# Reordering the first and the last token blocks of a fused attention and feed-forward layer on one core

## The chip, the cores and the metric

The kernel runs on one core of a Trainium2 chip. The metric is the device time of one execution in microseconds. The kernel before takes 528.72 us as the median of 3 runs (527.85 to 529.94). A profile of one further execution is the source of every duration used below.

## The reference

The input is x, 4 x 2048 tokens of 256 features in float32, treated here as 8192 tokens. One layer is computed:

```python
Q, K, V = x @ W_q.T, x @ W_k.T, x @ W_v.T
# chunks of 32 tokens, mask[i, j] = decay ** (i - j) for i >= j, else 0
S = einsum('bncd,bnkd->bnck', Qc, Kc) * mask
O = einsum('bnck,bnkd->bncd', S, Vc)
out = (sigmoid(x @ W_g.T) * O) @ W_o.T + x
h = layernorm(x + out)
gate, up = h @ wg.T, h @ wu.T            # int weights times 1/127, hidden size 768
y = (silu(gate) * up) @ wd.T
result = layernorm(h + y)
```

`decay` is the sigmoid of one scalar that arrives by DMA.

## The kernel before, in words

The 8192 tokens are cut into 16 blocks of 512 (`TB`), numbered 0 to 15. All blocks run through the same stages, written out by Python without a hardware loop. `in_turn` and `in_steady_turn` pin an instruction's place in the program order of its engine; unpinned ones are placed by a scheduler when the program is built, so every engine's stream is fixed before the kernel runs.

**Products in three passes.** Most matrix products split both operands into `hi`, `lo` and `gap` parts (`weight_parts`, `weight_up`, `weight_gap`, `token_parts`, L436 to L490). `three` (L526) first issues the hi and lo products of both of its PSUM banks, scales each bank by `WHOLE` on ScalarE (L536), and later, when the caller calls the function it returned, issues the gap products (the third pass) and the finishing copy. In what follows "the first passes" are the hi and lo products and "the gap pass" is the third. The tiles are `p_g` (the gate product), `p_v` (V), `p_y` (x times W_q.T W_k, used for the scores) and `p_o` (the output projection). GpSimd makes the lo parts (L452, L476), VectorE the gaps of tokens (L482).

**Per block.** `attn_scores` (tile `ps`, L647) multiplies yT with xT on TensorE and the mask on VectorE into `sT`; `attn_values` (tile `po`, L669) multiplies with V, and VectorE applies the gate into `goT`. `split_out` adds the residual, and `moments` (L341, L342) takes mean and variance. The norm is applied on ScalarE by `normalize` (L429), from a scale and a shift that either come from a Sqrt on ScalarE (`root`, L350) and a reciprocal on VectorE, or, in `iterated_scale_and_shift` (L404 to L418), from a power and one Newton step on GpSimd alone. A Sqrt on ScalarE costs two table loads, one before it and one in `back_to_silu` (L940). The normed block is transposed: by TensorE in `transpose_h` (tile `pt`) for blocks 0 and 15, otherwise by `move_h` (L781, L788), which transposes 32 x 32 squares on VectorE and then issues 16 DMAs on SP's queue, tile `hT`, and `split_h` (L805, L806).

**Feed-forward.** `ffn_up` (L823 to L846) runs 6 chunks of 128 hidden features per block: 8 matmuls into `fg` and `fu`, a Silu on ScalarE (`s`), a product on VectorE (`u`), a rounded copy on ScalarE (`u_hi`, L845) and its remainder on GpSimd (`u_lo`, L846). `ffn_down` (tile `fdn`) multiplies u with the third weight; with `chunkwise` it takes the first four chunks of both banks first ("early") and the last two after that ("late").

**Head.** Before the data arrive, matmuls of zeros warm TensorE up (tile `pi`, L190, widths in `WARM`). Block 0's gate, V and y products are plain float32 (`pg`, `pv`, `py`). `make_mask` (L255 to L270) raises the decay to 0..31 by repeated squaring, 18 small VectorE operations behind the 15 that prepare the bits, into `chunk_mask` and `mask`. Block 0's norm uses `root` and then four VectorE operations on h (L922). The integer weights are cast by `cast_fg`, `cast_fu`, `cast_fd` on ScalarE, three operations of about 0.55 us to a call.

**Loop.** For b = 0 to 13, block b's feed-forward chunks are interleaved with block b+2's attention and block b+3's first products.

**Tail.** Iteration b = 13 has no block b+3. After it, blocks 14 and 15 run their feed-forward parts, the last four groups of tokens are normed one after another, and the stores end the kernel.

Of the kernel before, what the change touches and what calls it, by code (L numbers as in the profile page):

```python
# [54 lines left out]
P = 128  # L55
# [14 lines left out]
SHIFT = 2.0**12  # L70
TOP = 1.0 - 0.5 / SHIFT
WHOLE = 1.0 + 1.0 / SHIFT
WARM = 512, 512, 128


@with_exitstack
def kernel(
# [32 lines left out]
    sums = ctx.enter_context(tc.tile_pool(name="sums", bufs=1))  # L110
    small = ctx.enter_context(tc.tile_pool(name="small", bufs=8))
    psum = ctx.enter_context(tc.tile_pool(name="psum", bufs=8, space=bass.MemoryType.PSUM))

    def bank(name):
        return psum.tile([P, TB], F32, tag="ps", name=name)
# [116 lines left out]
        )  # L232
    chunk_mask = const.tile([P, CHUNK], F32, tag="chunk_mask", name="chunk_mask")
    nc.vector.tensor_scalar(chunk_mask, diff, 0.0, None, ALU.is_ge)
    bits = []
    for i in range(CHUNK.bit_length() - 1):
        bit_int = setup.tile([P, CHUNK], I32, tag="bit_int", name=f"bit_int_{i}")
        nc.vector.tensor_scalar(
            bit_int, diff, i, 1, ALU.logical_shift_right, ALU.bitwise_and
        )  # L240
        bit, factor = (
            setup.tile([P, CHUNK], F32, tag=f"{tag}_{i}", bufs=1, name=f"{tag}_{i}")
            for tag in ("bit", "factor")
        )
        nc.vector.tensor_copy(bit, bit_int)
        nc.vector.tensor_scalar(factor, bit, -1.0, 1.0, ALU.mult, ALU.add)
        bits.append((bit, factor))
    mask = const.tile([P, NG, PAIR], F32, tag="mask", name="mask")
    nc.vector.memset(mask, 0.0)

    def in_turn(ins):
        tc.keep_in_program_order(ins)

    def make_mask():
        in_turn(nc.scalar.activation(decay, decay, AF.Sigmoid))  # L255
# [73 lines left out]
    def in_steady_turn(ins):  # L329
        if steady:  # L330
            tc.keep_in_program_order(ins)
# [4 lines left out]
    def moments(r, name, groups=range(NG), order=free, mv=None):  # L336

        mv = no_moments(name) if mv is None else mv
        for g in groups:
            st = small.tile([P, 6], F32, tag="st", name=f"st_{name}_{g}")  # L340
            order(nc.vector.bn_stats(st, r[:, g, :]))  # L341
            order(nc.vector.bn_aggr(mv[:, g, :], st))  # L342
        return mv
# [9 lines left out]
        )  # L353
        return std

    def layer_norm(r, name, on_r=1.0, on_dst=1.0):


        mv = moments(r, name)
        rstd = root(mv, name, on_r)  # L360
        nc.vector.reciprocal(rstd, rstd)
        if on_dst != on_r:
            nc.vector.tensor_scalar(rstd, rstd, on_dst / on_r, None, ALU.mult)
        for g in range(NG):
            nc.vector.tensor_scalar(
                r[:, g, :],
                r[:, g, :],
                mv[:, g, 0:1],
                rstd[:, g : g + 1],
                ALU.subtract,  # L370
                ALU.mult,
            )
# [343 lines left out]
    def attn_residual(b, goT):  # L716

        xn = xns.pop(b)
        r = norm.tile([P, NG, D], F32, tag="h", name=f"h_{b}")

        def residual(gs, pb):
            in_steady_turn(nc.vector.tensor_tensor(flat(r, gs), pb, flat(xn, gs), ALU.add))

        project_back(b, (chunked(goT),), (chunked(given["wo"]),), residual, "pa")
        return r

    def attn_out(b, goT):
        r = attn_residual(b, goT)
        layer_norm(r, f"a{b}", on_r=HALF, on_dst=H_UP)
        return r  # L730

    def split_out(b, go_parts):

# [75 lines left out]
        return hi, lo  # L809


    def ffn_up(b, hT, uT, chunks, cols=slice(0, TB), held=False):

        n = cols.stop - cols.start
        for hc in chunks:
# [14 lines left out]
                        in_turn(product)  # L830
            s = work.tile([P, n], F32, tag="s", name=f"s_{b}_{hc}")
            in_turn(nc.scalar.activation(s, pg, AF.Silu, scale=SCALE / H_UP))  # L832
            if len(uT[0]) == hc:
                for kind, dtype, tiles in zip(("hi", "lo"), (F32R, F16), uT):
                    tiles.append(
                        acts.tile([P, TB], dtype, tag=f"u_{kind}", name=f"u_{kind}_{b}_{hc}")
                    )

            def multiply(hc=hc, pu=pu, s=s):
                u = work.tile([P, n], F32, tag="u", name=f"u_{b}_{hc}")  # L840
                in_steady_turn(
                    nc.vector.scalar_tensor_tensor(u, pu, U_UP / H_UP, s, ALU.mult, ALU.mult)  # L842
                )
                hi, lo = uT[0][hc][:, cols], uT[1][hc][:, cols]
                in_steady_turn(nc.scalar.copy(hi, u))  # L845
                nc.gpsimd.tensor_tensor(lo, u, hi.bitcast(F32), ALU.subtract)  # L846

            if held:
                return multiply
# [81 lines left out]

    table = const.tile([P, 1], F32, tag="table", name="table")
    given = {"wg": wg, "wv": wv, "wo": wo}
    hs, hTs = {}, {}

# [3 lines left out]

    weight_parts(wg, "wg", ("wg_hi", "wg_lo"))
    make_mask()
    weight_parts(wv, "wv", ("wv_hi", "wv_lo"))
    back_to_silu()
    sg, gate = attn_gate(0)
    x_parts, x_gaps = token_parts(xTs[1], "x_1")

    def with_m():
        make_m()  # L950
        given["m"] = m_sb
        weight_parts(m_sb, "m", ("wq", "wk"))

    v, copies = attn_v(0, with_m)
    weight_up("wg")
    gate()
    copies()
    yT = attn_y(0)
    weight_gap("wg")
    weight_up("wv")  # L960
    weight_gap("wv")
    in_turn(nc.scalar.mul(wo, wo, HALF**2))
    weight_parts(wo, "wo", ("wo_hi", "wo_lo"))
# [4 lines left out]
    fg, cast_fg = integers(ffn_gT, ffn_int[0], "fg")  # L968
    fu, cast_fu = integers(ffn_uT, ffn_int[1], "fu")
    fd, cast_fd = integers(ffn_dT, ffn_int[2], "fd")  # L970
    cast_fg(0)
    v_1, rest = split_v(1, x_parts)
    look_up([0])
    cast_fg(1)
    sT = attn_scores(0, yT)
    xTs[2] = load_xT(2)
    g_rest()
# [1 line left out]
    look_up([1, 2])  # L979
    yT, rest = split_y(1, x_parts)  # L980
    goT = attn_values(0, sT, v, sg)
    rest()
    cast_fu(0)
    x_parts, x_gaps = token_parts(xTs[2], "x_2")
    hs[0] = attn_residual(0, goT)
    sT_1 = attn_scores(1, yT)
    xTs[3] = load_xT(3)
    mv = moments(hs[0], "a0", order=in_turn)
    weight_up("wo")
    weight_gap("wo")  # L990
    std = root(mv, "a0", HALF, order=in_turn)
    back_to_silu()
    v, rest = split_v(2, x_parts)
    x_gaps()
    goT = attn_values(1, sT_1, v_1, sg_1)
    in_turn(nc.vector.reciprocal(std, std))
    in_turn(nc.vector.tensor_scalar(std, std, H_UP / HALF, None, ALU.mult))
    for g in range(NG):
        scaled(hs[0], g, mv, std)
    go_parts, go_gaps = token_parts(goT, "go_1")  # L1000
    cast_fu(1)
    rest()
    yT, rest = split_y(2, x_parts)
    hTs[0] = transpose_h(0, hs[0])
    go_gaps()
    rest()
    look_up([3])
    hs[1], out_rest = split_out(1, go_parts)
    sg, g_rest = split_gate(2, x_parts)
    cast_fd(0)  # L1010
    scales_h = iterated_scale_and_shift(out_rest(), of_h, "h_1")
    ahead = yT, v, sg


# [7 lines left out]
    for b in range(NB - 2):  # L1022
# [7 lines left out]
        if b:  # L1030
            normalize(hs[b + 1], *scales_h)
        up_now(b, hT, uT, 0)
        if b == 0:
            g_rest()
            cast_fd(1)
            x_parts, x_gaps = token_parts(xTs[m], f"x_{m}")
        up_now(b, hT, uT, 1)
        if b:
            moving = move_h(b + 1, hs[b + 1])
        sT = attn_scores(n, yT)  # L1040
        if m + 1 < NB:
            xTs[m + 1] = load_xT(m + 1)
        up_now(b, hT, uT, 2)
        if b == 0:
            x_gaps()
            normalize(hs[b + 1], *scales_h)
            moving = move_h(b + 1, hs[b + 1])
        if more:
            v_next, v_rest = split_v(m, x_parts)
            up_now(b, hT, uT, 3)  # L1050
            v_rest()
            if scales_out is not None:
                normalize(r_before, *scales_out)
                store(b - 2, r_before)
        goT = attn_values(n, sT, v, sg)
        if b == 0:
            look_up(range(4, n_pieces))
        if b == 1:
            count = count_wide()
            n_wide_early = const.tile([1, 1], I32, tag="n_wide_early", name="n_wide_early")  # L1060
            nc.vector.tensor_copy(n_wide_early, count)
# [33 lines left out]
            if b:  # L1095
                scales_out = scale_and_shift(mv_before, std_before, of_out, f"out_{b}")
        else:
            std_out = root_in_turn(mv_out, of_out, f"out_{b}")
            back_to_silu()
            hs[n], out_rest = split_out(n, go_parts)  # L1100
            scales_out = scale_and_shift(mv_out, std_out, of_out, f"out_{b}")
            normalize(r_before, *scales_out)
            store(b - 1, r_before)

# [26 lines left out]
    def up_beside(b, uT, hc, r, groups, cols=slice(0, TB)):  # L1131
# [2 lines left out]
        normalize(r, *scales_out, groups)  # L1134
        multiply()

    ffn_up(last - 1, hTs[last - 1], uT, range(0, 1))
    up(last - 1, uT, 1, 3)
    hTs[last] = transpose_h(last, hs[last], 1)
# [3 lines left out]
        store_groups(last - 2, r_out, groups)  # L1143
    up(last - 1, uT, 5, KH)
    up(last, uT_last, 0, 1)
    r_before, mv_before, _ = ffn_down(last - 1, uT, hs[last - 1], chunkwise=True)
    scales_out = iterated_scale_and_shift(mv_before, of_out, f"out_{last - 1}")
    up(last, uT_last, 1, KH - 3)
    up_beside(last, uT_last, KH - 3, r_before, range(0, per))
    for g in range(per):  # L1150
        store_groups(last - 1, r_before, [g])
# [121 lines left out]
    def wide_block(start, weights):  # L1273
# [5 lines left out]
        gate()  # L1279
        copies()  # L1280
        goT = attn_values("w", attn_scores("w", attn_y("w")), v, sg)
        h = attn_out("w", goT)
        hT = moved.tile([P, KD, TB], F32, tag="hT", name="hT_w")
        for dc in range(KD):
            pt = bank(f"pt_w_{dc}")
# [110 lines left out]
```

## Time and profile before

| What | Value |
|---|---|
| median of 3 runs | 528.72 us |
| the profiled execution's own time | 528.65 us |
| its span, first to last instruction | 527.0 us |
| TensorE busy (PE) | 506.6 us, 96% |
| ScalarE busy (ACT) | 379.1 us, 72% |
| VectorE busy (DVE) | 312.4 us, 59% |
| GpSimd busy (POOL) | 286.3 us, 54% |
| granted TensorE clock, mean | 0.991 |

PEld is the load of weights into TensorE. "SPq" is SP's DMA queue. Times in the views count from the span's start. In a timeline row the columns are the start, the length of the merged instructions, the engine, line, operation, output and inputs, the count, and in brackets the idle time ahead of it on its engine with what ended it. A row that merges several instructions runs from the first one's start to the last one's end.

### The profile page before, as it was taken

Reading aid. Unit: us, or ns where it says so; the run is one execution under the profiler, and the core shown is the slowest. Engines: PE = TensorE matmul, PEld = TensorE weight load, DVE = VectorE, ACT = ScalarE, POOL = GpSimd, SP = SyncE. Lnnn points to the kernel's source line nnn. Section 1 sums busy time; section 2 is a strip of 40 time slices with the busy share of each in tenths; the row PEclk is TensorE's granted clock in tenths of the full one; section 3 lists DMA queues with packets and bytes.
Section 4 is the critical chain, followed back from the end, with each engine's and each line's share of the span. In section 5 each row is a group of like instructions: output and inputs, shape, how many; then the busy total and the mean of one; then the engine's idle time right before and its main releaser. Section 6 shows DMA issues by size and latency. Waiting matters only on the chain.

```text
span 527.0 us, 9688 instructions
## 1 busy us (share of the span) xinstructions
PE 506.6 (96%) x3480; PEld 400.3 (76%) x3480; DVE 312.4 (59%) x730; ACT 379.1 (72%) x705; POOL 286.3 (54%) x313
## 2 busy tenths in 40 slices
PE   9898899999999999999999999999999999997993
PEld 5686587787878878787887878788787878775772
DVE  4968576565474647547464754746475474655454
ACT  5858767676868777686877768687776868766754
POOL 4521654564646557474655747465574746365662
PEclk9999999999999999999999999999999999998997
DMA  8620211212222122212212222221322212021101
GB/s 264 188 106 3 81 40 41 76 47 58 63 84 77 42 76 86 63 60 86 77 41 78 83 62 61 85 76 41 80 81 60 64 45 77 1 57 65 40 27 56
DMA packets 43314, 36.83 MB, mean 70 GB/s; under 512 B 4864, under 2 KB 39168, under 8 KB 43264
## 3 DMA queue, kind: packets, MB, share of 16 engines
q1 hardware_dynamic: 42144, 35.28, 22.5%
q10 hardware_dynamic: 1120, 0.92, 0.5%
q8 instruction: 28, 0.46, 0.4%
q14 instruction: 22, 0.18, 0.1%
HBM read 20.45 MB, written 8.39 MB: 55 GB/s over the span
## 4 chain that ended last, share of the span: by engine, by line
PE 78%; DVE 6%; ACT 4%; SPq 3%; issue 2%; POOL 1%; DMA 1%; ACTq 0%; DVEq 0%
PE fg L823 15%; PE fu L823 14%; PE fdn L700 12%; PE p_y L495 7%; PE p_o L517 7%; PE p_g L495 7%; PE p_v L517 6%; PE po L669 4%; SPq L788 3%; PE ps L647 3%; DVE u L842 1%; PE fdn L889 1%; DVE st_a L341 1%; DMA hT<-sq 1%; ACT h L429 1%
## 5 line engine op out<-in xcount | busy, mean ns | idle before, releaser
L846 POOL TENSOR_TENSOR u_lo<-u,u_hi 128x512 f16<-128x512 f32 (+1 forms) x98 | 129.4, 1321 | 106.8 <-ACT u_hi L845 106.8
L842 DVE SCALAR_TENSOR_TENSOR u<-fu,s 128x512 f32<-128x512 f32 (+1 forms) x98 | 66.7, 681 | 131.9 <-ACT s L832 111.8
L845 ACT CAST u_hi<-u 128x512 fp32r<-128x512 f32 (+1 forms) x98 | 59.8, 611 | 89.3 <-DVE u L842 89.2
L823 PE MATMUL fg<-hT_hi,fg_hi 128*128 128x512 f32 (+1 forms) x196 | 71.4, 445 | 0.0
L823 PE MATMUL fu<-hT_hi,fu_hi 128*128 128x512 f32 (+1 forms) x196 | 60.6, 390 | 0.0
L832 ACT ACTIVATE s<-fg 128x512 f32<-128x512 f32 (+1 forms) x98 | 56.9, 580 | 4.2 <-PE fg L823 4.0
L823 PE MATMUL fg<-hT_lo,fg_lo 128*128 128x512 f16 (+1 forms) x196 | 58.1, 378 | 0.0
L823 PE MATMUL fu<-hT_lo,fu_lo 128*128 128x512 f16 (+1 forms) x196 | 57.4, 375 | 0.0
L476 POOL TENSOR_TENSOR go_lo<-goT,go_hi 128x512 fp32r<-128x512 f32 x30 | 37.9, 1283 | 30.7 <-ACT go_hi L475 30.7
L476 POOL TENSOR_TENSOR x_lo<-xT,x_hi 128x512 fp32r<-128x512 f32 x30 | 37.8, 1279 | 20.2 <-ACT x_hi L475 20.2
L700 PE MATMUL fdn<-fd_hi,u_hi 128*128 128x256 f32 x312 | 44.7, 285 | 0.0
L740 DVE TENSOR_TENSOR h<-p_o,x 128x512 f32<-128x512 f32 x30 | 19.4, 687 | 42.1 <-PE p_o L517 38.5
L823 PEld LDWEIGHTS fu<-hT_hi,fu_hi 128*128 128x128 f32 x196 | 36.5, 188 | 8.5
L823 PEld LDWEIGHTS fg<-hT_hi,fg_hi 128*128 128x128 f32 x196 | 34.5, 189 | 9.7 <-DVE hT_lo L765 0.3
L700 PEld LDWEIGHTS fdn<-fd_hi,u_hi 128*128 128x128 f32 x312 | 39.0, 188 | 0.3
L700 PE MATMUL fdn<-fd_lo,u_lo 128*128 128x256 f16 x312 | 38.6, 273 | 0.0
L429 ACT ACTIVATE h<-h,shift_h,scale_h 128x256 f32<-128x256 f32 x52 | 27.0, 590 | 16.0 <-POOL shift_h L392 16.0
L823 PEld LDWEIGHTS <-fu_lo 128*128 128x128 f16 x196 | 19.2, 98 | 22.2
L806 POOL TENSOR_TENSOR hT_lo<-hT,hT_hi 128x512 f16<-128x512 f32 x28 | 35.5, 1288 | 0.0
L669 PE MATMUL po<-sT,v 128*128 128x128 f32 x256 | 31.2, 275 | 1.0 <-DVE sT L659 1.0
L700 PEld LDWEIGHTS <-u_lo 128*128 128x128 f16 x312 | 28.4, 98 | 3.9
L669 PEld LDWEIGHTS po<-sT,v 128*128 128x128 f32 x256 | 30.0, 192 | 1.5 <-PE fu L823 1.4
(180 smaller groups left out, 1073.1 us busy)
## 6 DMA issues: line engine op xcount, KB each, us to landing
x<-in_x_dram SPq DMA_DIRECT2D x16, 512.0 KB, 3.5
xT<-in_xT_dram SPq DMA_DIRECT2D x15, 512.0 KB, 3.7
hT<-sq SPq DMA_DIRECT2D x224, 32.0 KB, 1.9
out_dram<-r SPq DMA_DIRECT2D x13, 512.0 KB, 3.1
out_dram<-r SPq DMA_DIRECT2D x7, 128.0 KB, 1.7
fg_int<-in_ffn_gT_dram SPq DMA_DIRECT2D x3, 256.0 KB, 8.2
fu_int<-in_ffn_uT_dram SPq DMA_DIRECT2D x3, 256.0 KB, 7.1
fd_int<-in_ffn_dT_dram SPq DMA_DIRECT2D x3, 256.0 KB, 5.9
```

Source lines behind the costliest of these rows:

```text
L429: nc.scalar.activation(r[:, g, :], r[:, g, :], AF.Identity, bias=shift[:, g : g + 1], scale=scale[:, g : g + 1],)
L476: in_turn(nc.gpsimd.tensor_tensor(lo[:, k, :], t[:, k, :], whole, ALU.subtract))
L495: nc.tensor.matmul(pb, lhsT=a[kind][:, k, i * P : (i + 1) * P], rhs=b[kind][:, k, :], start=kind + k == 0, stop=True, skip_group_check=True,)
L517: nc.tensor.matmul(pb[:, j * D : (j + 1) * D], lhsT=b[kind][:, k, g * P : (g + 1) * P], rhs=a[kind][:, k, :], start=kind + k + j == 0, sto ...
L669: product = nc.tensor.matmul(po[:, cols], lhsT=v[:, g, dc * P : (dc + 1) * P], rhs=sT[:, cols], start=True, stop=True,)
L700: product = nc.tensor.matmul(pb[:, j * D : (j + 1) * D], lhsT=part[:, g * P : (g + 1) * P], rhs=w, start=(i == 0), stop=(i == len(terms) - 1),
L806: nc.gpsimd.tensor_tensor(in_order[1], whole, in_order[0].bitcast(F32), ALU.subtract)
L823: product = nc.tensor.matmul(pb, lhsT=w[kind][:, dc, hc * P : (hc + 1) * P], rhs=hT[kind][:, dc, cols], start=(kind == kinds[0] and dc == ...
L832: in_turn(nc.scalar.activation(s, pg, AF.Silu, scale=SCALE / H_UP))
L842: nc.vector.scalar_tensor_tensor(u, pu, U_UP / H_UP, s, ALU.mult, ALU.mult)
L845: in_steady_turn(nc.scalar.copy(hi, u))
L846: nc.gpsimd.tensor_tensor(lo, u, hi.bitcast(F32), ALU.subtract)
```

## The change

In the head:

- `WARM` becomes one matmul of 512 columns and 22 of 32, instead of 512, 512 and 128.
- The sigmoid table is loaded by a dummy activation before the first weights arrive. `make_mask` stays behind the split of W_g, but the split of W_v moves behind the product M = W_q.T W_k, and block 0's gate (`gate()`) moves ahead of `token_parts` of block 1.
- Block 0's norm uses `iterated_scale_and_shift` (GpSimd) and `normalize` (ScalarE) in place of Sqrt, two table loads and four VectorE operations. Its moments are taken inside `attn_residual`, half by half.
- The casts of integer weights move later, block 2's gate product moves ahead of the gap pass of its y product, its gap pass into the head, and the split of block 3's tokens (`token_parts(xTs[3])`, with its gaps) moves ahead of block 0's feed-forward.
- In iteration 0, `normalize` of block 1 and its `move_h` move behind the first passes of block 3's V product.

In the last blocks:

- Iteration 13 issues block 15's scores after chunk 0 instead of after chunk 1.
- Iteration 13's last output norm uses `iterated_scale_and_shift` instead of Sqrt and two table loads.
- In blocks 14 and 15 (up to chunk 2 of block 15) the copy `u_hi` and remainder `u_lo` of a chunk are issued after the next chunk's Silu (`late_splits`, `lagging`).

The core of the diff:

```diff
-WARM = 512, 512, 128
+WARM = 512, *[32] * 22
...
+    table = const.tile([P, 1], F32, tag="table", name="table")
+    in_turn(nc.scalar.activation(table, eps, AF.Sigmoid))
     bits = []
...
     make_mask()
-    weight_parts(wv, "wv", ("wv_hi", "wv_lo"))
     back_to_silu()
     sg, gate = attn_gate(0)
+    gate()
     x_parts, x_gaps = token_parts(xTs[1], "x_1")
     def with_m():
         make_m()
         given["m"] = m_sb
+        weight_parts(wv, "wv", ("wv_hi", "wv_lo"))
         weight_parts(m_sb, "m", ("wq", "wk"))
...
-    cast_fg(0)
     v_1, rest = split_v(1, x_parts)
+    cast_fg(0)
...
+    cast_fg(1)
     rest()
+    x_parts, x_gaps = token_parts(xTs[2], "x_2")
     cast_fu(0)
-    x_parts, x_gaps = token_parts(xTs[2], "x_2")
-    hs[0] = attn_residual(0, goT)
+    x_gaps()
+    hs[0], mv = attn_residual(0, goT)
     sT_1 = attn_scores(1, yT)
...
-    std = root(mv, "a0", HALF, order=in_turn)
-    back_to_silu()
+    scales_h = iterated_scale_and_shift(mv, of_h, "h_0")
     v, rest = split_v(2, x_parts)
-    x_gaps()
+    cast_fu(1)
     goT = attn_values(1, sT_1, v_1, sg_1)
-    in_turn(nc.vector.reciprocal(std, std))
-    in_turn(nc.vector.tensor_scalar(std, std, H_UP / HALF, None, ALU.mult))
-    for g in range(NG):
-        scaled(hs[0], g, mv, std)
+    rest()
     go_parts, go_gaps = token_parts(goT, "go_1")
-    cast_fu(1)
-    rest()
-    yT, rest = split_y(2, x_parts)
+    yT, y_rest = split_y(2, x_parts)
+    normalize(hs[0], *scales_h)
+    go_gaps()
+    sg, g_rest = split_gate(2, x_parts)
+    y_rest()
     hTs[0] = transpose_h(0, hs[0])
-    go_gaps()
-    rest()
     look_up([3])
     hs[1], out_rest = split_out(1, go_parts)
-    sg, g_rest = split_gate(2, x_parts)
-    cast_fd(0)
+    g_rest()
+    x_parts, x_gaps = token_parts(xTs[3], "x_3")
     scales_h = iterated_scale_and_shift(out_rest(), of_h, "h_1")
+    x_gaps()
...  (the loop, b = 0 to 13)
         up_now(b, hT, uT, 0)
-        if b == 0:
-            g_rest()
-            cast_fd(1)
-            x_parts, x_gaps = token_parts(xTs[m], f"x_{m}")
+        if not more:
+            sT = attn_scores(n, yT)
         up_now(b, hT, uT, 1)
         if b:
             moving = move_h(b + 1, hs[b + 1])
-        sT = attn_scores(n, yT)
+        else:
+            cast_fd(0)
+        if more:
+            sT = attn_scores(n, yT)
...
-        if b == 0:
-            x_gaps()
-            normalize(hs[b + 1], *scales_h)
-            moving = move_h(b + 1, hs[b + 1])
         if more:
             v_next, v_rest = split_v(m, x_parts)
+            if b == 0:
+                normalize(hs[b + 1], *scales_h)
+                moving = move_h(b + 1, hs[b + 1])
             up_now(b, hT, uT, 3)
...
+            cast_fd(1)      (b == 0, behind attn_values and look_up)
...
         else:
-            std_out = root_in_turn(mv_out, of_out, f"out_{b}")
-            back_to_silu()
             hs[n], out_rest = split_out(n, go_parts)
-            scales_out = scale_and_shift(mv_out, std_out, of_out, f"out_{b}")
+            scales_out = iterated_scale_and_shift(mv_out, of_out, f"out_{b}")
...  (ffn_up)
             in_turn(nc.scalar.activation(s, pg, AF.Silu, scale=SCALE / H_UP))
+            no_more_splits()
...
-                in_steady_turn(nc.scalar.copy(hi, u))
-                nc.gpsimd.tensor_tensor(lo, u, hi.bitcast(F32), ALU.subtract)
+                def split():
+                    in_steady_turn(nc.scalar.copy(hi, u))
+                    nc.gpsimd.tensor_tensor(lo, u, hi.bitcast(F32), ALU.subtract)
+                if lagging:
+                    late_splits.append(split)
+                else:
+                    split()
```

`no_more_splits` issues what `late_splits` holds. `lagging` is on from block 14's chunk 0 to block 15's chunk 2; `no_more_splits` is also called ahead of block 14's `ffn_down` and behind block 15's chunk 2.

## The prediction

> **What bounds the kernel.** I read the page's slices first, then busy time by stretch, then the timeline where TensorE is idle.
>
> ```profile
> PE   9898899999999999999999999999999999997993
> PEclk9999999999999999999999999999999999998997
> ```
>
> TensorE is full from the seventh to the 36th of the 40 slices, so engines that finish earlier there give nothing, and the change leaves the order of instructions alone from block 1's chunks to the end of iteration 12. Only the two ends count.
>
> ```profile
> 20.00:30.00 10.00, 8.25 (x79) 7.16 (x79) 7.68 (x14) 8.77 (x18) 1.28 (x1) 1.00 0.18 56
> 40.00:50.00 10.00, 8.36 (x50) 7.05 (x51) 8.16 (x15) 8.46 (x18) 2.59 (x2) 1.00 0.01 2
> 60.00:70.00 10.00, 8.00 (x51) 6.47 (x51) 7.45 (x14) 7.62 (x16) 6.10 (x6) 1.00 0.10 30
> 470.00:480.00 10.00, 6.84 (x58) 6.26 (x57) 2.85 (x6) 8.31 (x16) 5.86 (x7) 1.00 0.23 72
> 480.00:490.00 10.00, 10.00 (x52) 7.24 (x51) 7.67 (x23) 4.52 (x10) 4.45 (x14) 0.83 0.16 55
> ```
>
> The second number behind the window is PE's busy time, the third from the end the granted clock. About 1.7 us is idle in each of the first two, 2.0 in the third, 3.2 in the fourth; the fifth is busy, but at a lower clock. The timeline shows what ended each wait (in brackets):
>
> ```profile
> 0.97 0.50 PEld L190 LDWEIGHTS pi<-const-float32-0.0 128*128 128x128 f32 x2 [0.97 <-issue]
> 4.55 0.34 PEld L190 LDWEIGHTS pi<-const-float32-0.0 128*128 128x128 f32 x1 [0.52 <-issue]
> 5.66 0.19 PEld L579 LDWEIGHTS pg<-xT,wg 128*128 128x128 f32 x1 [0.35 <-issue]
> 14.35 1.28 DVE L264 TENSOR_TENSOR power<-power 128x1 f32<-128x1 f32 x1
> 22.65 0.20 PEld L647 LDWEIGHTS ps<-yT,xT 128*64 128x64 f32 x4 [1.70 <-DVE yT L608]
> 41.21 1.01 PEld L517 LDWEIGHTS p_v<-wv_gap,x_gap 128*128 128x128 f32 x8 [1.94 <-ACT p_v L536]
> 45.76 0.30 PEld L495 LDWEIGHTS p_y<-x_gap,m_gap 128*128 128x128 f32 x2 [0.18 <-ACT p_y L536]
> 66.04 1.00 PEld L517 LDWEIGHTS p_v<-wv_gap,x_gap 128*128 128x128 f32 x8 [1.36 <-ACT p_v L536]
> 475.42 1.28 ACT L350 ACT_TABLE_LOAD   x1
> 477.03 1.28 ACT L940 ACT_TABLE_LOAD   x1
> 479.06 1.11 PEld L517 LDWEIGHTS p_o<-wo_gap,go_gap 128*128 128x128 f32 x8 [3.44 <-ACT p_o L536]
> 502.39 0.11 PEld L889 LDWEIGHTS <-u_lo 128*128 128x128 f16 x2 [0.89 <-POOL u_lo L846]
> ```
>
> **Warm-ups: +3.2 us (0 to +3.6, and a cold case among the rivals).** A float32 matmul is two passes, each with its own weight load, so 22 matmuls are 44 passes. The first 512 takes two passes of 0.85 us, to 2.70. A pass of 32 columns cannot be shorter than its load. From idle, the second p_y load starts 0.30 - 0.19 = 0.11 us after the first; the second pi load 0.50 - 0.33 = 0.17 us after the first, while 128-column pi passes were 0.21 apart. Between pi's and pg's third pass the spacing goes from 0.85 to 0.43 us, with one of 0.69 between, so TensorE speeds up at 5.50 (the clock row of the page does not show this, the spacing does). At 0.17 that is 16.5 passes until 5.50, then 27.5 x 0.108 = 3.0: the warm-ups end near 8.5 (8.8 at 0.21). The gate products then start there instead of 4.97, and end 8 x 0.43 later, at 11.9 instead of 8.67. TensorE's work is solid from there to 21, so this counts in full. If only the columns counted (32/128 of 0.21 each), they would end at 5.05 and cost 0. I take the loads.
>
> The Trainium skill (TensorE: Matmul & The Clock Gate, "LDWEIGHTS (loading the stationary operand)") gives a load as columns / 1.2 ns, 107 ns, at either clock. By it the warm-ups would end at 7.4, this term be 2.2 and the sum below 522.9. The same page ("What's actually happening") calls the warm-up a budget of time, not a number of matmuls, which speaks against any that runs on past 5.5.
>
> **Mask ahead of the splits: -1.8.** Small VectorE operations take 0.15 to 0.25 us alone and 1.2 to 1.3 beside GpSimd's (row 14.35), so the mask ends at 21.9, the yT copies follow, and the scores run 22.66 to 24.22 instead of from 21.0 for 1.15: 2.07 lost. After: decay lands 5.9 us behind its issue at 2.37, at 8.3; GpSimd then has only W_g's split, over before 8, until block 1's x, behind 11. The mask is done by 15. New is that sT of block 1 queues behind eight moments operations and x_gap on VectorE: 0.25 us. The W_v split moved behind M is needed 5 us later than it ends: 0.
>
> **Block 0's norm without tables: -1.75.** TensorE stood from 39.46 to 41.21 because the p_v scalings queue behind Sqrt and two loads. They now follow wo_lo and are done before TensorE arrives. GpSimd's chain for the norm (block 1's ran from 54.74 to 57.43, 2.7 us) has 3 us of cover: the gap pass of p_v and the first passes of p_y.
>
> **Transposes of block 0: -0.8.** They waited for h and took 1.75 us of TensorE with what follows, against 0.87. Now the normalize follows p_y's scalings on ScalarE and ends near the time at which the moved gate product (1.85 us of cover) ends. Without that cover TensorE would stand 1.85 longer.
>
> These sum to -4.35 before block 0's chunks, whose start T0 was 51.48.
>
> **Block 0's chunks: +1.36, no gain.** Here 2.1 us (x_hi, x_lo of block 3) and 1.1 us (p_v scalings) of waits go. But what ends last is another chain: normalize of block 1, its transposes, 16 DMAs of 0.64 us on SP's queue, hT_hi, and queued behind that on ScalarE the p_g scalings. From first DMA to the p_g gap pass it took 66.02 to 79.36, 13.34 us. Normalize began at T0 + 11.96. After, ScalarE does x_hi (1.15), s and u_hi of chunk 0 (u_0 on VectorE now behind x_gap, at T0 + 4.75), chunk 1, fd_hi (1.65), chunk 2, both p_v scalings (1.05): T0 + 12.4, and the p_g gap pass at T0 + 28.3 against 27.88. The block-2 gap pass (0.94) moved ahead of T0, so against equal work it is 1.36 later. TensorE could be there at about T0 + 25.9 and stands 2.4 us, in two pieces. Head: 3.2 - 4.35 + 1.36 = +0.2.
>
> The casts moved on ScalarE, look_up on VectorE, the x load behind xT on SP: 0, each has over 2 us to spare by the rows after it.
>
> **Iteration 13: -4.45.** Scores ahead of chunk 1: the 1.1 us stand at 463 (0.96 by PE's own record) goes, since sT follows u_0 now; the DMAs of block 14 move by +0.2 (transposes behind u_1 as before, but sT ahead). hT_hi thus still ends at 475.6, and the p_o scalings follow at once instead of behind 2 x 1.28 of loads. The gap pass starts at 476.2, not 479.06. TensorE then waits 1.65 us instead of 3.4. After the 3.15 us the clock was 0.50 from 480 to 483.5 and the 24 passes lost 1.7 us; after the 1.75 us at 39.5 it stayed 1.00, so I drop the 1.7 too. Chunk 0 of block 14 starts at 478.9 instead of 483.45: -4.55. GpSimd's power chain (2.45 us) now stands ahead of u_lo_5 and hT_lo; they end at 476.6 and 479.15, needed at 477.8 and 479.85: 0, but with 0.7 us of cover. Then h of block 15 arrives only at 485.3 (9.1 us behind the gap pass, as before), so the transposes end 0.6 later than that, and chunk 3 waits 0.3 for u_0 to free a bank: 3.65 left. The lagging copies give some back. ScalarE's cycle per chunk was s 0.59, a wait of 0.81 for u, u_hi 0.62, more than TensorE's 1.87; interleaved it is 1.2, and of the 0.89 us at 502.39 for u_lo 0.8 goes: 4.45 in all. A lagging copy is queued behind the next Silu, which waits for TensorE's next chunk; only `ffn_down` reads it, and u_lo_5 is there at 497.2, needed at 497.8. u of chunk k+2 waits for u_lo of chunk k to free its buffer, at most 0.9 us, while the banks still last: 0.
>
> **End: -0.5.** s of block 15's chunk 2 no longer waits for u_hi of chunk 1, and the ScalarE chain is 0.8 us earlier; the last u_lo held TensorE 0.5 us at 517.2.
>
> Sum, against the profiled 528.65 (median 528.72, so alike): 528.65 + 0.2 - 4.45 - 0.5 = **523.9 us**.
>
> **Rivals.**
>
> *Warm-ups cost only their columns* (term 0): 520.7. Against it stand the 0.11 and 0.17 us between loads. Chance 0.13.
>
> *The stand in block 0 slows the clock.* 2.4 us lies between 1.75 (clock kept) and 3.15 (lost, 1.7 us): 525.6. Chance 0.14; for it, both pieces lie within 5 us.
>
> *Short warm-ups don't warm.* TensorE multiplies for 0.05 of each 0.17 to 0.21 us. If that doesn't count as activity, 44 x 0.21 = 9.4 us of cold passes end at 12.1, and the next 4.5 us (as in the first stretch) run at half speed, losing 2.25: the gate products end at 17.8, the term is 9.1, the total 529.8, slower than before. It decides from a term of 8.0. For it: the profile shows no dense loads with short matmuls; against it: the first 1.7 us are dense, and half of it would give 527. Chance 0.16, split about evenly between 527 and 530.
>
> *Half of the 4.45 is taken back*, by hT_lo or u_lo_5 behind the power chain or by h of block 15: 526.1. For it: covers of 0.6 and 0.7 us. Chance 0.1.
>
> **Numbers.** The forecast's own case (522.8 to 524.9) has 0.47. The range, 520.6 to 528.8, reaches over the free warm-ups, the lost clock and half of the cold case. 0.5% (2.6 us) is about what a measurement of this kernel can tell from no change. Faster, below 526.0: the forecast 0.47, the free warm-ups 0.13, of the lost clock 0.09, of the halved tail 0.03: 0.72. Slower, above 531.3: half of the cold case, with a further wait, 0.08. Within: 0.2.
>
> **What would show it.** Right: pg's first pass near 8.5, one pi pass each 0.17 then 0.11; VectorE's mask copies before 16; no wait ahead of block 0's ps; no table loads between 12 and 80; p_g's gap pass of block 3 waiting for ScalarE near 79.5 with hT_hi just ahead; no stand over 2 us near 475, clock 1.00 there. Wrong: pg near 5 (free), matmuls of 0.85 us behind 9 (cold), a clock of 0.50 near 80, hT_lo ending after fg's hi passes of block 14.

## The result, and the profile after

The changed kernel takes 536.14 us (median of four runs, 534.32 to 536.97) against 529.25 for the kernel before: ratio 1.0129, interval 1.0094 to 1.0164. It is slower, 12 us above the forecast and 7 above the top of the range. The profiled execution took 536.97 us, with a span of 535.4.

The first view is again the page's slices. The hole at the seventh digit of PE is a new one, and the clock there is 0.7.

```profile
PE   9998996999999999999999999999999999998993
PEclk9999997999999999999999999999999999998997
```

Next, busy time by stretch (PE's busy time second, the granted clock third from the end). From 40 to 50 TensorE is idle for 1.5 us. Block 0's chunks now lose 4.1 us and then run at half clock; iteration 13 still loses 2.2, with the half clock behind it.

```profile
40.00:50.00 10.00, 8.48 (x84) 7.65 (x84) 7.95 (x17) 4.66 (x10) 5.29 (x10) 1.00 0.36 108
80.00:90.00 10.00, 5.89 (x30) 4.91 (x29) 3.77 (x6) 5.30 (x11) 6.03 (x5) 0.80 0.12 28
90.00:100.00 10.00, 10.00 (x68) 8.56 (x67) 7.98 (x23) 6.13 (x11) 3.87 (x5) 0.85 0.16 52
480.00:490.00 10.00, 7.82 (x60) 7.21 (x59) 3.71 (x6) 6.20 (x13) 7.13 (x11) 0.94 0.28 80
490.00:500.00 10.00, 10.00 (x54) 7.06 (x53) 7.72 (x23) 4.77 (x10) 5.28 (x16) 0.89 0.16 54
```

The timeline shows where each begins: TensorE's matmuls first, then the weight loads that had to wait, then what they waited for.

```profile
1.00 11.27 PE L193 MATMUL pi<-const-float32-0.0 128*128 128x512 f32 x46 [1.00 <-PEq L1397]
12.08 6.53 PE L583 MATMUL pg<-xT,wg 128*128 128x512 f32 x8
18.45 1.89 PE L625 MATMUL pv<-wv,xT 128*128 128x256 f32 x8
...
46.74 1.86 PEld L673 LDWEIGHTS po<-sT,v 128*128 128x128 f32 x16 [1.69 <-issue]
88.13 1.35 PEld L499 LDWEIGHTS p_g<-x_gap,wg_gap 128*128 128x128 f32 x4 [4.32 <-ACT p_g L540]
488.33 1.39 PEld L521 LDWEIGHTS p_o<-wo_gap,go_gap 128*128 128x128 f32 x8 [2.46 <-ACT p_o L540]
...
39.61 2.67 DVE L486 SCALAR_TENSOR_TENSOR x_gap<-x_hi,xT 128x512 fp32r<-128x512 f32 x2
45.78 0.84 DVE L663 TENSOR_TENSOR sT<-ps,mask 64x256 f32<-64x256 f32 x2
73.55 11.57 SPq L790 DMA_DIRECT2D hT<-sq  x16
86.46 1.14 ACT L807 CAST hT_hi<-hT 128x512 fp32r<-128x512 f32 x2 [3.07 <-DMA hT<-sq]
```

The warm-ups end at 12.08 instead of 4.97, and the eight gate passes behind them take 6.5 us instead of 3.9: they run at half speed, called cold below. A stand is a stretch in which TensorE runs nothing. The first V product starts at 18.45, 9.78 later than before. A landmark is the first matmul of one product in both profiles; the differences of its start, read along the program, place every gain and loss:

| step | forecast | measured |
|---|---|---|
| warm-ups, to the first V product | +3.2 | +9.78 |
| waits of the head, to block 2's scores | -4.35 | -3.36 |
| block 0, to block 3's p_g gap pass | +1.36 | +2.35 |
| clock behind it, to block 1's chunk 0 | 0 | +2.09 |
| blocks 1 to 12 | 0 | +0.55 |
| iteration 13, to block 14's chunk 0 | -4.55 | -2.16 |
| blocks 14 and 15, and the end | -0.4 | -0.78 |
| sum | -4.74 | +8.47 |

(The span grew from 526.95 to 535.42. The forecast's 0.9 for h of block 15, its 0.8 for the lag and its 0.5 for the end are in the last row.)

### The profile page after: what moved, and what is told of

Its sections match the earlier page's. It is cut to its first block, busy times and chain, and to the rows that moved or that the text cites. A ratio compares the mean times of both kernels' runs of the same rounds, so it can differ in the third digit from the quotient of the medians.

```text
span 535.4 us, 9771 instructions
## 1 busy us (share of the span) xinstructions
PE 516.6 (96%) x3520; PEld 411.6 (77%) x3520; DVE 304.3 (57%) x725; ACT 373.7 (70%) x701; POOL 292.4 (55%) x324
## 4 chain that ended last, share of the span: by engine, by line
PE 71%; DVE 8%; ACT 8%; SPq 6%; issue 3%; POOL 1%; DMA 1%; DVEq 0%; ACTq 0%
PE fg L831 12%; PE fu L831 11%; PE fdn L704 10%; PE p_g L499 6%; PE p_y L499 6%; PE p_o L521 6%; PE p_v L521 6%; SPq L790 6%; PE po L673 4%; DVE u L851 3%; PE ps L651 2%; PE pi L193 2%; PE fdn L905 2%; ACT s L840 2%; ACT h L433 1%
```

## The experiments

**The warm-ups, one way and the other.** First the changed kernel with the old list, and the kernel before with the new one.

```diff
-WARM = 512, *[32] * 22      (old_warm: in the changed kernel)
+WARM = 512, 512, 128
-WARM = 512, 512, 128        (short_on_before: in the kernel before)
+WARM = 512, *[32] * 22
```

> The changed kernel with the warm-ups of before (512, 512, 128) and nothing else altered. Theory A (the loss is the warm-ups alone: block 0's first V product began 9.78 us later than before, 18.45 instead of 8.67, and the whole kernel is 8.3 us longer): that 9.78 goes in full, the V product starts near 8.67, and the time is 536.1 - 9.8 = 526.4, ratio to before about 0.995. It still has the 4.3 us stand of TensorE in block 0 and the half clock behind it. Theory B (the late head had cover that is gone when the head is early, since waits on DMAs stand still): only 5 to 7 of the 9.8 come back, 529 to 531. Theory C (the half clock near 86 to 93 us came from the cold start): it goes too, 524.3.

> The kernel before with only the warm-ups changed to 512 and 22 of 32. Theory A: 44 passes 0.21 us apart at half speed to about 12.1, then seven passes of 0.85 on the gate product, first V product near 18.45 (+9.78); the waits of the head of before (on the mask and on the tables) hide nothing of it: 529.2 + 9.8 = 539.0. Theory B (the head of before waits for loads and for GpSimd, which a later TensorE covers): 534 to 537.

Alone in the kernel before, the short warm-ups cost 538.04 - 528.62 = 9.4 us (ratio 1.017, 1.015 to 1.019). That is near theory A's 9.8, but partly by luck. Against the profile of before, this run is 9.48 later at the first V product and only 7.33 later at block 2's scores, mainly since the wait for the mask, 1.49 us in before, is covered, as theory B had it. A DMA issue of 1.50 us in block 0 and the late landing of iteration 13's last transfer of h, for which ScalarE waits 0.81 us, then bring 0.92 and 0.94 back.

Without the short warm-ups the rest of the change is a gain: 523.2, ratio 0.9887 (0.9866 to 0.9908). That is 12.9 less than the changed kernel, 3.5 more than those 9.4, so no theory had it. The landmarks of the changed kernel and of old_warm place the difference: 9.04 at the first V product, 10.28 at p_g's gap pass, 10.88 at block 1, 11.08 at iteration 13, 12.03 at p_o's gap pass, 13.60 at block 14. Both jumps, 1.24 and 0.95, lie in a chain of 16 DMAs, and a loss of clock follows each, which costs 0.60 and 1.57 more than in old_warm. (In block 0 old_warm loses the clock too, and 1.5 us by it.)

**Too long, or cold?** Three other lists in the changed kernel, each apart from the others in one thing.

```diff
+WARM = 512, *[32] * 6       (few_short)
+WARM = (512,) * 10          (long_warm)
+WARM = 512, *[128] * 22     (mid_warm)
```

> The changed kernel with warm-ups of one 512 and six of 32: 12 short passes, ending near 5.4 at 0.21 apart, about when the warm-ups of before ended (4.97). Theory A (TensorE speeds up only after 4.5 to 5.9 us of passes of full length on end, and short ones start the count anew): the gate product's passes are 0.85 apart from 5.4 to about 11.3, the V product starts near 11.6, 2.9 later than with the old warm-ups: 529.3. Theory A2 (short passes only halt the count, the 1.7 us of the first 512 are kept): speeds up near 8.2, V product near 10.2, +1.6: 528.0. Theory B (time from the first matmul counts, whatever its length): speeds up at 5.5 as before, V product near 9.1: 526.9.

> The changed kernel with ten warm-ups of 512, 20 passes. They should be 0.85 us apart until 5.5 and 0.43 from there, and end near 11.8, close to where the 44 short passes ended (12.1). Theory A (length and coldness are two costs): the gate product runs at 0.43 per pass, the V product starts near 15.3, 6.6 later than with the old warm-ups and 3.2 earlier than with the short ones: about 533. Theory B (only the length of the warm-ups counts, and the slow gate product is its own affair, as every first real product is slow): V product near 18, 536.

> The changed kernel with 22 warm-ups of 128 columns instead of 32: as many instructions on TensorE, and as long a cold pass (0.21 us, as the 128-column passes of before show), but TensorE multiplies all the time. Theory A (it is the share of time in which TensorE multiplies that opens the clock): the passes go from 0.21 to 0.11 apart between 3.9 and 7.0, as in the runs so far, the warm-ups end near 8.9, the gate product's passes are 0.43 apart and block 0's first V product starts near 12.3 (11.5 to 13.1), 6 us earlier than with 32 columns. Theory B (the loads or the number of passes keep it cold): all as in the changed kernel, V product at 18.4, 536. For the time, two theories on the 3.5 us by which the changed kernel lost more than its 9.4 of warm-ups: theory C (the load of TensorE's own code, one 16 KB packet per some 255 of its instructions, stretches one issue of an hT DMA from 0.6 to 1.5 or 1.8 us in block 0 and in iteration 13, and where it falls is set by the count of TensorE's instructions, which is the same here): both chains again hold such an issue, 530.9. Theory D (where it falls is set by the late start, not by the count): 526.7.

mid_warm has the passes of the changed kernel, at the same 0.21 us, but a pass of 128 columns multiplies through all of it:

```profile
1.00 7.92 PE L193 MATMUL pi<-const-float32-0.0 128*128 128x512 f32 x46 [1.00 <-PEq L1397]
8.76 3.60 PE L583 MATMUL pg<-xT,wg 128*128 128x512 f32 x8
12.19 1.89 PE L625 MATMUL pv<-wv,xT 128*128 128x256 f32 x8
```

The spacing drops from 0.21 to 0.11 at 4.9, the gate product runs warm in 3.6 us and V starts at 12.19, as theory A had it. Number of passes and loads are the same, so what keeps TensorE cold goes with the columns: 32 of 128, and it multiplies for a quarter of the time. (No run has short passes that lie closer together, so the share and the length of a pass are not told apart.) long_warm's 20 long passes reach 0.43 at 4.0, and V starts at 14.59, 3.9 earlier than with 44 short ones that end 0.9 later. In few_short, 12 short passes end at 5.26, yet the gate passes are 0.85 apart until 10.3: V at 11.25, where theory A had 11.6, A2 10.2 and B 9.1. What lay ahead of the gate product did not help, as A said; but nothing starts a count anew, the last section shows a grid of windows instead. Its time, 523.9, is only 0.7 above old_warm: its profile is 1.84 later at V and 0.29 at block 1, since there the clock survived the stand in block 0.

So the 9.78 are two costs: 7.11 of warm-ups that end later, and 2.67 of gate passes at half speed.

**Where the other 3.5 us came from.** A DMA issue on SP's queue takes 0.6 us. In both chains of the changed kernel one takes longer, just as a packet of the instruction queue q8, 16 KB, moves. One timeline line, then the queue table of the stretch around it (packets, MB, share of 16 engines):

```profile
80.72 1.84 SPq L790 DMA_DIRECT2D hT<-sq  x1
...
q8 instruction: 1, 0.02, 4.2%
```

In the 14 profiles 97 of 3,136 issues of hT took more than 0.85 us, and each of the 97 has a q8 packet during it or at most 0.7 us ahead of it. q8 carries 29 such packets over the kernel, 18.8 us apart in the mean. Between two of them TensorE executes some 255 matmuls and loads, 225 to 310; ScalarE's count goes from 18 to 45. So they look like the load of TensorE's own code, which is inferred from these counts alone. The changed list adds 80 instructions, so by this estimate each packet falls about 80/255 x 18.8 = 5.9 us earlier against the work; with the old list it comes at 80.3, when the last issue of the chain is over (74.84). The same happens at 482.8, in iteration 13 (1.55 us). mid_warm, with as many instructions and a head 6 us earlier, has its long issues at the very same DMAs, the 33rd and the 278th of the queue (1.61 and 1.57 us): the count of TensorE's instructions sets them, theory C. Its 529.12 lies between C and D, the mechanism is C's. long_warm agrees: its V is later still, 14.59 against 12.19, but with 52 instructions fewer it has no long issue in either chain, and its time, 529.83, is 3 below its theory A.

**The chain in block 0.** In old_warm the p_g gap pass still waits 3.05 us. Here the normalize goes ahead.

```diff
-            cast_fd(0)                          (iteration 0, behind chunk 1)
+            normalize(hs[b + 1], *scales_h)
         if more:
             sT = attn_scores(n, yT)
+        if b == 0:
+            moving = move_h(b + 1, hs[b + 1])
...
-                normalize(hs[b + 1], *scales_h)  (behind split_v)
-                moving = move_h(b + 1, hs[b + 1])
+                cast_fd(0)
```

> The kernel with old warm-ups (523.2), and in iteration 0 normalize of block 1 ahead of the scores of block 2 and its move to hT directly behind them, in the place of the cast of fd_hi, which takes normalize's old place behind the first passes of block 3's V product. Theory A (the chain normalize, 16 DMAs, hT_hi, p_g scalings ends last in block 0): the first DMA goes 4 us earlier, p_g's gap pass waits for nothing, the stand of about 3 us and the half clock behind it (1.5 us lost between 77.85 and 86.86) go, 0.4 is lost as normalize is longer than the cast: 519.1. Theory B (the stand goes but the clock is lost anyway, from the other short waits of block 0): 520.6. Theory C (fd_hi later holds up chunk 3 and the go_hi split, the wait moves there): 522 to 523.5.

It takes 519.75 (ratio 0.9824, 0.9805 to 0.9843), theory A. One line of old_warm, one of early_norm:

```profile
77.85 0.30 PEld L499 LDWEIGHTS p_g<-x_gap,wg_gap 128*128 128x128 f32 x2 [3.05 <-ACT p_g L540]
```

```profile
74.97 0.30 PEld L499 LDWEIGHTS p_g<-x_gap,wg_gap 128*128 128x128 f32 x2 [1.00 <-ACT p_g L540]
```

The wait falls to 1.00 instead of to nothing; the clock stays at 1.00.

**Iteration 13 and the head.** Two more moves, each on top of the one before.

```diff
+        if not more:                             (early_norm_move)
+            moving = move_h(b + 1, hs[b + 1])
         up_now(b, hT, uT, 0)
...
-    x_gaps()                                     (all_moves: the head)
     hs[0], mv = attn_residual(0, goT)
     sT_1 = attn_scores(1, yT)
+    x_gaps()
```

> The one before this, and in iteration 13 move_h of block 14 ahead of chunk 0 instead of behind chunk 1. The 16 DMAs then start some 4.8 us earlier and hT_hi is no longer what the p_o scalings queue behind. Theory A (the stand of about 1.6 us that is left ahead of p_o's gap pass goes): 517.5. Theory B (go_lo and go_gap or GpSimd end as late as hT_hi did, or VectorE's transposes now hold u_0 and the scores): 518.5 to 519.5.

> The one before this, and the gap split of block 2's tokens (x_gaps) issued behind the scores of block 1 instead of ahead of block 0's output product. In the changed kernel VectorE did x_gap, 2.67 us, and eight moments operations ahead of sT of block 1, and TensorE stood about 1.5 us for it (45.1 to 46.77). Theory A (sT then ends 1.3 us earlier, and x_gap is still early enough for the gap pass of p_v): -1.2, 516.3. Theory B (the residual of block 0 is bound by TensorE's pa, so sT ends as late as before, or the wait moves to p_v's gap pass): -0.3 or nothing, 517.2 to 517.5.

The first gives 518.76, 1.0 less where theory A had 1.6, so the time is in theory B's range; but the stand goes as A had it, p_o's gap pass waits 0.20 instead of 1.50. The second gives 516.72, 2.0 less where theory A had 1.2 (516.3): a ratio of **0.9766 (0.9749 to 0.9783)** to the kernel before, and the fastest of the study.

```profile
PE   9999899999999999999999999999999999999993
```

> The kernel with the three moves (516.7) and the changed kernel's short warm-ups. Theory A (the short warm-ups cost 9.4, as they did in the kernel before, and the changed kernel lost 3.5 more only because its two hT chains ended last; here these have 3 us and more to spare): 516.7 + 9.4 = 526.1. Theory B (a late, cold start costs 3.5 more elsewhere): 529.6.

With the short warm-ups in that kernel the time is 525.33, 8.6 more, where theory A had 9.4 and B 12.9. The packets then come behind both chains, at 78.9 and 476.2, where the last issues end at 77.6 and 473.3, so no issue in them is stretched; that slack would cover one is not shown.

**The parts of the tail.** Undone all together in old_warm, then the scores alone there, then the lag alone in all_moves.

> The changed kernel with the warm-ups of before and its three tail edits undone: scores of block 15 behind chunk 1 again, the last output norm by Sqrt and two table loads again, copies of u at once. Theory A (the tail edits are worth what the landmarks of the kernel with old warm-ups show, 455.59 - 455.26 = +0.33 at the start of iteration 13 and -4.83 at the last down-product): 5.2 more than the 523.2 of that kernel, 528.4, so that the head edits alone are worth about nothing against before (the half clock near 80 to 87 takes what they save). Theory B (part of the tail is recovered by the end chain of the last block): 526 to 527.

> The kernel with old warm-ups (523.2) with block 15's scores behind chunk 1 again. Theory A (the prediction's: the 1.1 us stand ahead of po comes back and is paid): 524.3. Theory B (TensorE stands 1.6 us for hT_hi ahead of p_o's gap pass anyway, and with the scores behind chunk 1 the moves of h to hT are issued 0.6 earlier, so nothing is lost): 522.6 to 523.2.

> The kernel with the three moves and the copies of u at once again in blocks 14 and 15. Theory A (the lag is worth what the landmarks between block 14's down-product and block 15's chunk 1 show, 0.8 us): 517.5. Theory B (it is also worth something at the end, 0.5 as the prediction had it): 518.0. Theory C (with block 14's inputs earlier the copies are no longer late): 516.7.

no_tail takes 528.73: the three edits are worth 5.5 us, and the head edits without the warm-ups nothing against before (ratio 1.0002, 0.9988 to 1.0016), as most of their gain is lost again (by the landmarks 3.4 us gained to block 2's scores, then 1.1 lost in block 0's chain, 1.4 by its clock and 0.3 up to iteration 13). scores_back takes 523.12 against 523.2: the earlier scores are worth nothing (theory B). all_moves_nolag takes 518.33 against 516.72, so the lag is worth 1.6, more than any theory had (1.3). The lines of the all_moves_nolag timeline show what it removes: waits for u, the transposes' hT_lo and u_lo, one behind the other.

```profile
481.51 0.30 PEld L831 LDWEIGHTS fu<-hT_hi,fu_hi 128*128 128x128 f32 x2 [0.37 <-DVE u L851]
485.31 0.30 PEld L831 LDWEIGHTS fg<-hT_hi,fg_hi 128*128 128x128 f32 x2 [0.78 <-DVE hT_lo L767]
492.41 0.11 PEld L905 LDWEIGHTS <-u_lo 128*128 128x128 f16 x2 [0.89 <-POOL u_lo L857]
```

## Why the prediction was wrong

**The failed step is the warm-ups.** "At 0.17 that is 16.5 passes until 5.50, then 27.5 x 0.108 = 3.0": it took the moment at which TensorE speeds up from a head of long passes and let the short ones have it too. They were 0.21 us apart from first to last, and the 512 ahead of them ended at 2.84, not 2.70. The rival "short warm-ups don't warm" had the mechanism and the number (term 9.1, measured 9.78; gate products ending at 17.8, measured 18.45), with a chance of 0.16 and half of that at 527. The row that spoke for it was in the text, a pass that multiplies for 0.05 of 0.21 us; the argument against it, 1.7 dense us at the start, was worth nothing.

The rule weighed there, a load of 107 ns at either clock, fails too (the page's formula names no clock, so "at either" was the prediction's reading): cold, the short passes were 0.21 us apart, though they multiply for a quarter of that and had nothing but their loads besides. The sentence of the Trainium skill (TensorE: Matmul & The Clock Gate, "What's actually happening") that the warm-up is a budget of time and not a number of matmuls was right to speak against the list, and these runs add that the time must be spent multiplying. The page's window runs freely, so the point varies; here TensorE sped up 3.0 to 6.0 us after the first of a run of long passes, and with the old list V began anywhere from 8.05 to 9.41.

**Head: -3.36 for -4.35.** The mask was in time and block 0's scores waited for nothing; p_v's gap pass and the transposes did not wait either. The term that was mis-sized is sT of block 1, put at 0.25: behind x_gap (2.67 us) and eight moments operations it held TensorE 1.5 us (its row ends at 46.62, po's loads start at 46.74). all_moves gets that back.

**Block 0: mechanism right, two sizes off.** In old_warm the chain cost +1.10 against +1.36 forecast. TensorE stood 2.84 us ahead of p_g's gap pass and 1.20 ahead of p_v's, 13.4 us earlier, against 2.4 in two pieces. In the changed kernel the stretched issue added 1.24, which no step of the prediction had. "The stand slows the clock" was a rival at 0.14; it happened behind six of the seven such stands in block 0, in the seven profiles that have the change's head and its order of block 0.

**Iteration 13: -4.45 was right, in old_warm** (-4.68 to block 14's chunk 0, forecast -4.55; the stand 1.23 us, forecast 1.65; clock 1.00). In the changed kernel the stretched issue made it 2.18, the clock was lost, and 2.2 us remained of the gain. The feared covers (hT_lo, u_lo_5, h of block 15) held. The lag was put at 0.8 plus 0.5 at the end; together it is 1.6.

With the warm-ups' true cost alone, the forecast would have been 530.5. The rest of the miss, 6.6 by the two profiles (5.6 by the medians), is the two stretched issues (2.2), the clock lost behind the stands (2.1 in block 0, of which old_warm has 1.5 without a stretched issue, and 1.6 in iteration 13), sT and the head's remainder (1.0) and a drift in the middle (0.55), less some 0.8 that block 0's chain and the tail gave beyond their terms; what causes the drift was not tried.

## What to carry to other kernels

A warm-up has to multiply nearly all the time: long matmuls, and only until the first real operands land, since real products warmed TensorE as well (at 10.3 in few_short). A stand of TensorE can cost more than its own time: when it fills half of one of the windows below, the clock goes too, and another 1.2 to 2.7 us with it. Where a chain of DMAs ends last, 80 instructions more on TensorE moved a q8 packet into it, so give such chains an early start instead of a tight one.

## What had not been expected of the hardware

- **When the clock is lost.** All 14 profiles together: stands of up to 1.83 us kept it. Stands of 2.18 and 2.20 lost it; of five stands of 2.84 to 2.89 four lost it and one (few_short) kept it; all five from 3.15 to 4.11 lost it. The Trainium skill (TensorE: Matmul & The Clock Gate, "HAM oscillation — how this bites in real kernels") warns of idle gaps over some 3.4 us; here 2.2 is enough.
- **What decides is how a stand lies in a grid.** In each of the 14 profiles every change of the granted clock lies a whole number of 3.413 us from the one at the start. Cut into such windows, the profiles agree without exception. At full clock, windows in which TensorE was idle for up to 1.70 us kept it, and those with 1.75 or more lost it at their end. At half clock, windows with up to 0.56 us without multiplying opened it, those with 0.68 or more did not (a short warm-up counted for a quarter of its time). So few_short kept its clock by luck: its stand of 2.84 us fell on a border, 1.70 and 1.14. The two windows of old_warm, then those of few_short, PE's busy time second and the clock third from the end:

```profile
75.25:78.66 3.41, 0.81 (x3) 0.59 (x4) 0.00 (x0) 2.48 (x5) 2.24 (x3) 1.00 0.04 10
78.66:82.08 3.42, 3.42 (x16) 3.17 (x15) 1.67 (x3) 3.40 (x7) 1.95 (x2) 0.50 0.02 5
...
75.11:78.52 3.41, 1.71 (x15) 1.51 (x13) 1.60 (x3) 1.15 (x3) 2.10 (x2) 1.00 0.16 39
78.52:81.94 3.42, 2.28 (x15) 1.90 (x16) 0.48 (x1) 3.42 (x9) 2.52 (x2) 1.00 0.00 0
```

- **A code load shows up on another engine's queue.** Per some 255 instructions of TensorE there is one 16 KB packet, and a DMA issue on SP's queue at that moment takes 0.9 to 1.8 us instead of 0.6.
- **The clock row does not show the cold start.** It reads 1.00 from 10 to 20 us in the changed kernel, while passes of 512 columns were 0.85 apart until 17.8; of the views, the spacing alone tells.
